# Reordering the opening of a cross-attention kernel: the first block's norm in two halves, mask rows on another queue, values in three row pairs

## The chip, the cores and the metric

The kernel runs on one core of a Trainium2 chip, as one program with one launch. The metric is the device time in microseconds (us), the median of several runs. The engines are TensorE (PE), VectorE (DVE), ScalarE (ACT), GpSimd (POOL) and SyncE (SP, which here only issues DMAs). Each works through its own list of instructions in order and waits on semaphores for the others.

## The reference

For x of 2048 tokens by 256 features and a context of 1601 rows by 192 features with a mask (float32 throughout):

```
xn  = layer_norm(x, g_norm)
q   = xn @ Wq                       # 16 heads of 64
k,v = split(context @ Wkv)          # 16 heads of 64
k,v = null key and value in front   # 1602 keys
s   = (q * scale) @ k^T, masked     # softmax over the keys
x   = x + layer_norm(softmax(s) @ v @ Wout, g_out)
h   = layer_norm(x), then three layers with weights of +1 or -1 (256 -> 1024 -> 1024 -> 256)
out = x + scaled h
```

## The kernel before

The sixteen heads are eight pairs (`NP`), the tokens four blocks of 512 (`NB`). The 32 units of the main loop (L681) are all pairs by all blocks, the block running fastest. A unit has 13 steps, one for each tile of 128 keys. A step makes scores for two heads on TensorE (L442), takes their exponential on ScalarE (`exps`, L468) and forms one chunk of the row maxima of the *next* unit (`max_chunk`, L376: two TensorE matmuls, L400, and one VectorE reduction, L403). GpSimd sums the exponentials into `acc` (L720, L722, L728). After the steps come the weighted values (L475), the output projection of the unit before, the query projection of the unit after next, and a part of the next pair's keys or values (L796): in blocks 0 and 1 the keys, in block 2 the first eight value tiles, in block 3 the last five. The feed-forward layers follow the last unit.

All this is under an order written out by hand. Each engine executes its instructions in the order in which the program text issues them. Two pools of PSUM buffers, `flex` and `spare`, have two buffers each of two banks; a new tile waits until the readers of the tile two back in its pool are done. `slot` alternates between the two pools by a counter, `n_slots`.

The opening (L566 to L678) has no unit before it to hide behind. It issues the loads, waits for the first block of x, norms it (`input_root` L538, `input_normed` L542, which centres four token tiles on VectorE at L91), turns it with eight transposes on TensorE (`input_turned`, L550) into `xnT`, and makes the first pair's keys (`first_keys`, L234, in four chunks), its queries (`first_queries`, L216, in two halves of 256 tokens) and its values (`values_begun` L300, `values_ended` L314). It then makes all 13 chunks of unit 0's maxima, combines them (`max_combined`, into `mcol`), turns them (`max_turned`, the matmul `mt` at L413), and starts the first exponential. `second_summed` and `second_normed` norm the second block of x on ScalarE and GpSimd. `keys_stepped` (L291) and `values_masked` (L360) work on the first pair's keys and values on GpSimd. `REST` is the last chunk of the maxima, of 66 keys for all four token tiles.

Before any data have landed, TensorE does 11 matmuls on the identity into a tile that nobody reads (`idle`, L633 to L635; 22 passes in the profile, since a float32 matmul shows as two). They wait for the identity, which GpSimd makes (`make_identity`, L580).

The context has 192 features: 128 in `ctx_a`, and the other 64 in `ctx_b`, held twice, in the lower and the upper 64 partitions. A matmul over 64 rows uses half of TensorE's rows, so two that use different halves (rows 0 to 63 and 64 to 127) and different banks run side by side: a row pair. (In the opening's timeline the 16 passes of eight value tiles over 128 rows, at 18.20, take 2.05 us, and the 16 passes over 64 rows as four such pairs, at 20.75, 1.05 us.) Value tile t takes its half by its bank, `(t - 8 * m) // 4`. The last five value tiles (8 to 12) lie with four in the first bank and one in the second, so one row pair and three single matmuls.

`keep` is the mask as one row on each partition, loaded with a broadcast; `kept` holds it by key tile; `masked_counted` (L425) sums it on TensorE into `spent`. `seen` (L708, L711) is a copy on ScalarE of one element of the last accumulator: after it, the exponentials of this unit need no wait of their own on GpSimd. It is made at step 2 in most units and at step 8 in the others:

```
if k == (2 if 2 < u < len(units) - 4 else 8) and last is not None:
    nc.scalar.copy(seen[:, 1:2], last[3][:1, 0, 0:1])
```

Of the kernel before, what the change touches and what calls it, by code (L numbers as in the profile page):

```python
# [21 lines left out]
CD = 192  # L22
# [16 lines left out]
def xattn_ffn(ctx, tc, x, ctxT, mask, g_norm, null_kv, wq, wkv, wout, g_out, k0, k1, k2, s0, s1, s2, out):  # L39
# [52 lines left out]


    norms = {}
    n_slots = 0

    def slot(name):
        nonlocal n_slots
# [49 lines left out]
    with ExitStack() as att:  # L148
# [19 lines left out]

        weights = {}

        def load_pair(p):
            wq_t = pp.tile([128, 2, 128], F32, tag="wq", name=f"wq_{p}")
            wa_t = pp.tile([128, 2, 128], F32, tag="wa", name=f"wa_{p}")
            wb_t = pp.tile([128, 2, 128], F32, tag="wb", name=f"wb_{p}")
            wo_t = lp.tile([128, D], F32, tag="wo", name=f"wo_{p}")
            both = wkv.rearrange("r (k w) -> r k w", k=2)[:, :, ts(p, 128)]
            nc.sync.dma_start(out=wa_t, in_=both[0:128])
            nc.sync.dma_start(out=wb_t[:64], in_=both[128:CD])
            nc.sync.dma_start(out=wb_t[64:], in_=both[128:CD])
            nc.sync.dma_start(out=wq_t, in_=wq[:, ts(p, 128)].rearrange("(c r) w -> r c w", c=2))  # L180
            if p > 0:
                nc.sync.dma_start(out=wo_t, in_=wout[ts(p, 128), :])
            weights[p] = (wq_t, wa_t, wb_t, wo_t)
# [50 lines left out]
        def first_keys(n, get, part=None):  # L234

            kT, _, kr = pairs[0]
            chunks = (CHUNKS[1], CHUNKS[2]) if n == 1 else (CHUNKS[n],)
            if part != 1:
                halves["k"] = get(f"psk_0_{n}")
            ps = halves["k"]  # L240
            for i, (start, w) in enumerate(chunks):
                if part is None or part == i:
                    nc.tensor.matmul(
                        ps[:, i, :w], weights[0][1][:, 0, :], ctx_a[:, ds(start, w)], start=True, stop=False
                    )
            if part == 0:
                return
            for i, (start, w) in enumerate(chunks):
                rows = ts(i, 64)
                nc.tensor.matmul(  # L250
                    ps[:, i, :w], weights[0][2][rows, 0, :], ctx_b[rows, ds(start, w)], start=False, stop=True
                )
            for i, (start, w) in enumerate(chunks):
                for part in range(2 if n == 0 else 1):
                    keys = ds(256 * part, 256) if n == 0 else ds(start, w)
                    relative(kT, ps[:, i, ts(part, 256)] if n == 0 else ps[:, i, :w], keys)
                    if n == 0 and part == 0:
                        nc.scalar.copy(kr[:, keys], kT[:, keys])
                    else:
                        nc.gpsimd.tensor_copy(kr[:, keys], kT[:, keys])  # L260
            if n == 3:
                nc.vector.memset(kT[:, KEYS:], 0.0)
# [34 lines left out]

        halves = {}

        def values_begun(p, m, tiles, get=flex):  # L300

            if (p, m) not in halves:
                halves[p, m] = get(f"psv_{p}_{m}").rearrange("p i (t d) -> p (i t) d", d=128)
            for t in tiles:
                nc.tensor.matmul(  # L305
                    halves[p, m][:, t - 8 * m, :],
                    ctx_a[:, ts(t, 128)],
                    weights[p][1][:, 1, :],
                    start=t % 4 == 0,
                    stop=False,  # L310
                    skip_group_check=True,
                )

        def values_ended(p, m):  # L314

            v, pv = pairs[p][1], halves[p, m]
            tiles = range(8 * m, min(8 * m + 8, KC))
            for t in sorted(tiles, key=lambda t: (t % 4, t)):
                rows = ts((t - 8 * m) // 4, 64)
                nc.tensor.matmul(  # L320
                    pv[:, t - 8 * m, :],
                    ctx_b[rows, ts(t, 128)],
                    weights[p][2][rows, 1, :],
                    start=False,
                    stop=True,
                    skip_group_check=True,
                )
            w = len(tiles)
            nc.scalar.copy(v[:, ds(8 * m, w), :], pv[:, :w, :])
            if p > 0 and m == 0:  # L330
                nc.gpsimd.tensor_copy(v[0:1, 0, :], nullv)

        def project_v(p, m):

            values_begun(p, m, range(8 * m, min(8 * m + 8, KC)))
            values_ended(p, m)

        def second_summed():

# [82 lines left out]
        def rows_of(k):  # L422
            return 128

        def masked_counted(get):  # L425

            ps = get("count")
            nc.tensor.matmul(ps[:, 0, :KC], ones_r.bitcast(F32), kept, start=True, stop=True)
            nc.vector.tensor_reduce(spent, ps[:, 0, :KC], AX.X, ALU.add)
            nc.gpsimd.tensor_scalar(spent, spent, float(KEYS), ident[:, KLAST : KLAST + 1], ALU.subtract, ALU.mult)  # L430
            for row in range(64, KLAST):
                nc.gpsimd.tensor_tensor(spent, spent, ident[:, row : row + 1], ALU.add)
# [105 lines left out]
        def input_root(b):  # L538
            mv = stats(x_sb[:, ts(b, 4), :], 4, f"x{b}")
            return mv, input_scale(b, mv)  # L540
# [35 lines left out]
            engine.dma_start(out=ctx_b[:64, ds(at + skip, w - skip)], in_=ctxT[128:CD, ds(at + skip - 1, w - skip)])  # L576


        nc.gpsimd.memset(keep[:, 0:1], 0)
        make_identity(nc, ident)  # L580
        nc.gpsimd.dma_start(out=gn_sb, in_=g_norm.rearrange("(c p) -> p c", p=128))
        for j in range(2):
            nc.gpsimd.dma_start(out=nullk[ts(j, DH), :], in_=null_kv[0].rearrange("(p o) -> p o", o=1))
        nc.gpsimd.dma_start(out=keep[:, 1:], in_=mask.partition_broadcast(128))
        for t in range(4):
            (nc.sync, nc.scalar)[t % 2].dma_start(out=x_sb[:, t, :], in_=x[ts(t, 128), :])
        load_context(nc.scalar, 0)
        load_pair(0)
        load_context(nc.sync, 1)
        at, w = CHUNKS[2]  # L590
        nc.sync.dma_start(out=ctx_a[:, ds(at, w)], in_=ctxT[0:128, ds(at - 1, w)])
# [34 lines left out]
        nc.scalar.activation(warm, eps_sb, AF.Sqrt)  # L626

        open_pair(0)
        xn = input_root(0)

        input_normed(0, *xn)

        idle = slot("idle")  # L633
        for _ in range(11):
            nc.tensor.matmul(idle[:, 0, :128], ident, ident, start=True, stop=True)  # L635
        input_turned(0, spare)
        first_keys(0, flex)
        first_queries(0)
        max_chunk(0, 0, 0)
        max_chunk(0, 0, 3)  # L640
        first_queries(1)
        nc.gpsimd.tensor_copy(kept[:, : KC - 1], mcol_u8[:, : KC - 1])
        nc.gpsimd.tensor_copy(kept[:KLAST, KC - 1 : KC], mcol_u8[:KLAST, KC - 1 : KC])
        mv, r = second_summed()
        max_chunk(0, 0, 6)
        first_keys(1, spare, 0)
        max_chunk(0, 0, 9)
        first_keys(1, spare, 1)
        values_begun(0, 0, range(0, 8), spare)
        max_chunk(0, 0, 1)  # L650
        nc.vector.reciprocal(r, r)
        second_normed(mv, r)
        nc.scalar.activation(warm, eps_sb, AF.Exp)
        max_chunk(0, 0, 4)
        values_ended(0, 0)
        max_chunk(0, 0, 7)
        first_keys(3, spare)
        max_chunk(0, 0, 10)
        values_begun(0, 1, range(8, KC), spare)
        max_chunk(0, 0, 2)  # L660
        values_ended(0, 1)
        max_chunk(0, 0, 5)
        keys_stepped(0)
        values_masked(0, 0)
        values_masked(0, 1)
        input_turned(1, spare)
        max_chunk(0, 0, 8)
        max_chunk(0, 0, 11)
        project_q(0, 1, spare)
        max_chunk(0, 0, REST)  # L670
        odd = spare("sT_0_0_1")
        sT = [spare("sT_0_0_0"), odd]
        scores(0, 0, 1, sT[1])
        max_combined(0, 0)
        max_turned(0, 0)
        scores(0, 0, 0, sT[0])
        masked_counted(flex)
        begin.__exit__(None, None, None)  # L678
        last = None
        with tc.manual_schedule():  # L680
            for u, (p, b) in enumerate(units):  # L681
# [25 lines left out]

                    nc.scalar.copy(seen[:, 0:1], before[:1, 0, 0:1])  # L708
                for k in range(KC):
                    if k == (2 if 2 < u < len(units) - 4 else 8) and last is not None:  # L710
                        nc.scalar.copy(seen[:, 1:2], last[3][:1, 0, 0:1])  # L711
                    if k == 0 and u > 0:

                        odd = spare(f"sT_{p}_{b}_1")
                        sT = [spare(f"sT_{p}_{b}_0"), odd]
                    es.append(exps(p, b, k, sT))
                    if nxt is not None:
                        max_chunk(*nxt, order[k])
                    if k == 2:
                        nc.gpsimd.tensor_tensor(acc, es[1], es[2], ALU.add)  # L720
                    elif 2 < k < 8:
                        nc.gpsimd.tensor_tensor(acc, acc, es[k], ALU.add)  # L722
# [231 lines left out]
```

## Time and profile before

| | |
|---|---|
| Runs | 1269.85, 1270.46, 1270.71 us |
| Median | 1270.46 us |
| Profiled execution | 1270.18 us, with a span of 1268.4 us |
| TensorE, GpSimd, VectorE, ScalarE busy | 99%, 80%, 60%, 57% of the span |
| First exponential of unit 0 | 34.65 us after the span's start |
| First exponential of unit 4, of unit 8 | 168.13, 300.19 us |

Times in the profile are counted from the start of the span. An engine's busy share is an average over the opening, the units and the feed-forward layers. In the timeline, a row's length runs from the start of the first of its instructions to the end of the last, and the number behind x counts them. Matmuls overlap, since one is issued before the one ahead of it has ended, so what an instruction costs TensorE is the distance between starts.

### The profile page before, as it was taken

How to read it: one execution, taken by the hardware profiler on the slowest of the kernel's cores; microseconds unless marked ns; L12 is line 12 of the kernel's file. 1: busy time of each engine (PE TensorE's matmuls, PEld its weight loads, DVE VectorE, ACT ScalarE, POOL GpSimd, SP SyncE). 2: the span in 40 equal slices, each digit the busy share in tenths (PEclk: the TensorE clock that was granted, in tenths of full speed). 3: DMA queues.
4: the chain of work that ended last, by engine and by line, in shares of the span. 5: the costliest groups of instructions: out<-in, count | busy, mean ns of one | idle time of the engine just before them, and what ended most of it. 6: DMA issues, size and time to landing. Idle time of an engine off the chain costs nothing.

```text
span 1268.4 us, 19642 instructions
## 1 busy us (share of the span) xinstructions
PE 1257.9 (99%) x8332; PEld 644.0 (51%) x8332; DVE 761.7 (60%) x812; ACT 717.9 (57%) x982; POOL 1008.5 (80%) x515
## 2 busy tenths in 40 slices
PE   8999999999999999999999999999999999999998
PEld 5344444444444444444444444444444443788887
DVE  6687766656665566556655666656666793635431
ACT  4776666666666656665666566666666676322120
POOL 5898999899889988998899988998898999701100
PEclk9999999999999999999999999999999999999999
DMA  6000000000000000000000000000000010000000
GB/s 171 1 1 5 1 1 13 5 1 1 13 5 1 1 14 5 1 1 13 5 1 2 13 5 1 1 1 6 1 17 1 1 42 1 1 17 1 17 17 17
DMA packets 16984, 13.46 MB, mean 11 GB/s; under 512 B 3152, under 2 KB 16336, under 8 KB 16896
## 3 DMA queue, kind: packets, MB, share of 16 engines
q1 hardware_dynamic: 15904, 11.21, 3.2%
q8 instruction: 65, 1.06, 0.4%
q10 hardware_dynamic: 656, 0.79, 0.2%
q0 software_dynamic: 336, 0.21, 0.1%
q14 instruction: 23, 0.19, 0.0%
HBM read 10.11 MB, written 2.10 MB: 10 GB/s over the span
## 4 chain that ended last, share of the span: by engine, by line
PE 95%; POOL 2%; ACT 1%; DMA 1%; issue 0%; DVE 0%; SPq 0%; DVEq 0%; POOLq 0%; ACTq 0%
PE sT L442 28%; PE av L475 27%; PE ps L836 12%; PE max L400 7%; PE psq L211 4%; PE po L488 4%; PE ps L867 2%; PE psv L305 2%; PE psk L270 1%; PE den L499 1%; PE sT L466 1%; PE psv L320 1%; POOL acc L728 1%; PE psk L275 1%; PE max L384 1%; PE mt L413 1%
## 5 line engine op out<-in xcount | busy, mean ns | idle before, releaser
L403 DVE TENSOR_REDUCE mx<-max 128x2 f32<-128x1024 f32 x384 | 444.4, 1218 | 86.0 <-PE max L400 82.3
L728 POOL TENSOR_TENSOR acc<-acc,e 128x1024 f32<-128x1024 f32 x192 | 473.1, 2464 | 15.1
L468 ACT ACTIVATE e<-sT 128x1024 f32<-128x1024 f32 x416 | 425.8, 1024 | 87.7 <-PE sT L466 44.3
L442 PE MATMUL sT<-qT,kT 64*128 64x512 f32 x1664 | 444.8, 608 | 1.6 <-ACT e L468 1.3
L722 POOL TENSOR_TENSOR acc<-acc,e 128x1024 f32<-128x1024 f32 x160 | 379.3, 2371 | 12.6
L475 PE MATMUL av<-e,v 128*32 128x512 f32 x3328 | 363.6, 592 | 0.1
L400 PE MATMUL max<-kr,qr 64*128 64x512 f32 x768 | 280.6, 718 | 1.2 <-ACT qr L227 1.0
L475 PEld LDWEIGHTS av<-e,v 128*32 128x32 f32 x3328 | 107.4, 110 | 237.9 <-issue 230.1
L442 PEld LDWEIGHTS sT<-qT,kT 64*128 64x128 f32 x1664 | 134.0, 185 | 132.6 <-ACT e L468 121.0
L720 POOL TENSOR_TENSOR acc<-e,e 128x1024 f32<-128x1024 f32 x32 | 75.6, 2363 | 59.6 <-ACT e L468 59.6
L400 PEld LDWEIGHTS max<-kr,qr 64*128 64x128 f32 x768 | 76.7, 187 | 88.6 <-DVE mx L403 65.2
L517 ACT COPY aoT<-r 32x256 f32<-32x256 f32 x224 | 90.2, 403 | 33.4 <-DVE r L511 31.1
L782 ACT COPY avs<-av 128x512 f32<-128x512 f32 x32 | 18.8, 587 | 145.8 <-PE av L475 145.8
L415 DVE TENSOR_TENSOR mT<-mt,pick 128x512 fp32r<-128x512 f32 x32 | 22.1, 690 | 113.4 <-PE mt L413 112.9
L518 DVE TENSOR_TENSOR aoT<-avs,aoT 128x512 f32<-128x512 f32 x28 | 33.3, 1189 | 94.4 <-ACT aoT L517 94.4
L836 PE MATMUL ps<-h0hi,w 128*128 128x512 f32 x256 | 79.6, 392 | 0.0
L836 PE MATMUL ps<-h0lo,w 128*128 128x512 f32 x256 | 78.9, 389 | 0.0
L124 POOL TENSOR_TENSOR y_sb<-y_sb,gout_sb 128x256 f32<-128x256 f32 x12 | 9.3, 777 | 85.6 <-DVE y_sb L91 85.6
L824 ACT ACTIVATE h1hi<-ps 128x1024 fp32r<-128x1024 f32 x16 | 16.4, 1027 | 99.2 <-PE ps L836 99.2
L212 ACT ACTIVATE qr<-psq 128x512 fp32r<-128x512 f32 x31 | 18.5, 598 | 93.5 <-PE psq L211 91.4
L488 PE MATMUL po<-wo,aoT 128*128 128x256 f32 x256 | 60.5, 379 | 0.0
L825 DVE SCALAR_TENSOR_TENSOR h1lo<-ps,h1hi 128x1024 fp32r<-128x1024 f32 x16 | 19.6, 1224 | 67.0 <-ACT h1hi L824 67.0
(171 smaller groups left out, 1207.8 us busy)
## 6 DMA issues: line engine op xcount, KB each, us to landing
out_x<-o SPq DMA_DIRECT2D x7, 256.0 KB, 2.1
x_sb<-in_x SPq DMA_DIRECT2D x3, 512.0 KB, 5.2
wa<-in_wkv SPq DMA_DIRECT2D x8, 128.0 KB, 2.9
wb<-in_wkv SPq DMA_DIRECT2D x16, 64.0 KB, 2.5
wq<-in_wq SPq DMA_DIRECT2D x8, 128.0 KB, 2.2
wo<-in_wout SPq DMA_DIRECT2D x8, 128.0 KB, 2.1
xnT<-in_k SPq DMA_DIRECT2D x1, 1024.0 KB, 5.7
ctx_a<-in_ctxT SPq DMA_DIRECT2D x2, 256.0 KB, 6.2
```

The lines of the kernel that those rows point to most:

```text
L211: nc.tensor.matmul(ps[:, 0, :], weights[p][0][:, c, :], xnT[:, b, c, :], start=c == 0, stop=c == 1)
L400: nc.tensor.matmul(ps[:, j, :w], qr[rows, ts(t, 128)], kr[rows, ds(start, w)], start=True, stop=True)
L403: nc.vector.tensor_reduce(maxima[p, b][:, t, :, c], ps[:, :, :w], AX.X, ALU.max)
L442: nc.tensor.matmul(ps[:n, j, :], kT[rows, ds(128 * KEY_TILES[k], n)], qT[rows, :], start=k < 2, stop=k >= 2, skip_group_check=k >= 2,)
L468: nc.scalar.activation(e, ps, AF.Exp)
L475: nc.tensor.matmul(av[ts(i, 32), 0, :], v[:n, KEY_TILES[k], ts(i, 32)], e[:n, i // 2, :], start=k == 1, stop=k == 0, tile_position=(0, 32 ...
L488: nc.tensor.matmul(pv[:, t, :], aoT[:, ts(t, 128)], weights[p][3], start=True, stop=True)
L517: nc.scalar.copy(aoT[ds(64 * j + 32 * rows, 32), ts(h, 256)], r[ds(64 * j + 32 * h, 32), :])
L720: nc.gpsimd.tensor_tensor(acc, es[1], es[2], ALU.add)
L722: nc.gpsimd.tensor_tensor(acc, acc, es[k], ALU.add)
L728: nc.gpsimd.tensor_tensor(acc, acc, es[k], ALU.add)
L836: nc.tensor.matmul(ps[:, f, :], w(c)[:, ts(2 * g + f, 128)], parts[part][:, c, :], start=i == 0, stop=i == len(steps) - 1,)
```

## The change

Six things are done, nearly all in the opening.

- GpSimd issues the loads of `gn_sb` and `nullk` ahead of the identity. The mask rows `keep` go from GpSimd's queue to SP's, behind the first half of the weights. Token tiles 2 and 3 of x are loaded after the first chunk of the context and most of pair 0's weights.
- The first block is normed and turned in two halves of two token tiles (`first_stats`, `first_centred`, `first_turned`). The first keys' first part stands ahead of the transposes in TensorE's list. The second half's reciprocal and centred tiles stand behind `max_chunk(0, 0, 0)` on VectorE; ScalarE does both scalings of its transposes.
- In the opening's second part, the chunks of keys, values and maxima are interleaved in another way; the Exp table is loaded after the first copy of values; REST comes before the second block's query projection.
- The last five value tiles lie as three and two in the two banks (`places`), for every pair: two row pairs and a single matmul. (In the opening too; the edit's name for it is three row pairs.) Their copy on ScalarE becomes two, of three tiles and of two.
- The count of the mask goes into the second bank of the last keys' tile, right behind them, rather than into a `flex` tile at the end.
- The `seen` copy of unit 28 is made at step 2 rather than 8. `n_slots` starts at 1 and `idle` is a `flex` tile, so `slot` alternates as it did.

The diff, with the definitions of two loads cut:

```
-    n_slots = 0
+    n_slots = 1
...
-            if part != 1:
+            if not part:
                 halves["k"] = get(f"psk_0_{n}")
...
-            if part == 0:
+            if part in (0, 1):
                 return
...
+        places = {t: t if t < 8 else t - 8 if t < 11 else t - 7 for t in range(KC)}
...
-            for t in sorted(tiles, key=lambda t: (t % 4, t)):
-                rows = ts((t - 8 * m) // 4, 64)
+            for t in sorted(tiles, key=lambda t: (places[t] % 4, t)):
+                rows = ts(places[t] // 4, 64)
...
-            w = len(tiles)
-            nc.scalar.copy(v[:, ds(8 * m, w), :], pv[:, :w, :])
+            for at, w in ((0, 8),) if m == 0 else ((8, 3), (11, 2)):
+                nc.scalar.copy(v[:, ds(at, w), :], pv[:, ds(places[at], w), :])
...
+        def first_stats(h):
+            mv = stats(x_sb[:, ts(h, 2), :], 2, f"x0{h}")
+            r = sp.tile([128, 4], F32, tag="rstd", name=f"rstd_x0{h}")
+            nc.scalar.activation(r[:, :2], mv[:, :2, 1], AF.Sqrt, bias=eps2_sb, scale=1.0 + EPS)
+            return h, mv, r
+        def first_centred(h, mv, r):
+            nc.vector.reciprocal(r[:, :2], r[:, :2])
+            for j in range(2):
+                centred(y_sb[:, 2 * h + j, :], x_sb[:, 2 * h + j, :], mv, r, j)
+        def first_turned(h):
+            pt = spare(f"xT_0_{h}")
+            cols = ts(h, 256)
+            for j in range(2):
+                for c in range(2):
+                    nc.tensor.transpose(pt[:, c, ts(j, 128)], y_sb[:, 2 * h + j, ts(c, 128)], ident)
+            nc.scalar.mul(xnT[:, 0, 0, cols], pt[:, 0, :256], gn_sb[:, 0:1])
+            if h == 0:
+                nc.vector.tensor_scalar_mul(xnT[:, 0, 1, cols], pt[:, 1, :256], gn_sb[:, 1:2])
+            else:
+                nc.scalar.mul(xnT[:, 0, 1, cols], pt[:, 1, :256], gn_sb[:, 1:2])
...
-        def masked_counted(get):
-            ps = get("count")
-            nc.tensor.matmul(ps[:, 0, :KC], ones_r.bitcast(F32), kept, start=True, stop=True)
-            nc.vector.tensor_reduce(spent, ps[:, 0, :KC], AX.X, ALU.add)
+        def masked_counted(ps):
+            nc.tensor.matmul(ps[:, 1, :KC], ones_r.bitcast(F32), kept, start=True, stop=True)
+            nc.vector.tensor_reduce(spent, ps[:, 1, :KC], AX.X, ALU.add)
...
-        nc.gpsimd.memset(keep[:, 0:1], 0)
-        make_identity(nc, ident)
         nc.gpsimd.dma_start(out=gn_sb, in_=g_norm.rearrange("(c p) -> p c", p=128))
         for j in range(2):
             nc.gpsimd.dma_start(out=nullk[ts(j, DH), :], in_=null_kv[0].rearrange("(p o) -> p o", o=1))
-        nc.gpsimd.dma_start(out=keep[:, 1:], in_=mask.partition_broadcast(128))
-        for t in range(4):
-            (nc.sync, nc.scalar)[t % 2].dma_start(out=x_sb[:, t, :], in_=x[ts(t, 128), :])
+        nc.gpsimd.memset(keep[:, 0:1], 0)
+        make_identity(nc, ident)
+        for t, engine in enumerate((nc.sync, nc.scalar)):
+            engine.dma_start(out=x_sb[:, t, :], in_=x[ts(t, 128), :])
+        load_pair(0, 0)
         load_context(nc.scalar, 0)
-        load_pair(0)
+        nc.sync.dma_start(out=keep[:, 1:], in_=mask.partition_broadcast(128))
+        load_pair(0, 1)
+        for t, engine in ((2, nc.sync), (3, nc.scalar)):
+            engine.dma_start(out=x_sb[:, t, :], in_=x[ts(t, 128), :])
+        load_pair(0, 2)
...
-        xn = input_root(0)
-        input_normed(0, *xn)
-        idle = slot("idle")
+        idle = flex("idle")
         for _ in range(11):
             nc.tensor.matmul(idle[:, 0, :128], ident, ident, start=True, stop=True)
-        input_turned(0, spare)
-        first_keys(0, flex)
+        first_centred(*first_stats(0))
+        first_keys(0, flex, 0)
+        first_turned(0)
+        first_keys(0, flex, 2)
         first_queries(0)
+        later = first_stats(1)
         max_chunk(0, 0, 0)
+        first_centred(*later)
         max_chunk(0, 0, 3)
+        first_turned(1)
         first_queries(1)
...
+        first_keys(1, spare, 0)
         mv, r = second_summed()
         max_chunk(0, 0, 6)
-        first_keys(1, spare, 0)
+        first_keys(1, spare, 1)
         max_chunk(0, 0, 9)
-        first_keys(1, spare, 1)
-        values_begun(0, 0, range(0, 8), spare)
+        first_keys(1, spare, 2)
+        values_begun(0, 0, range(0, 6), spare)
         max_chunk(0, 0, 1)
-        nc.vector.reciprocal(r, r)
-        second_normed(mv, r)
-        nc.scalar.activation(warm, eps_sb, AF.Exp)
+        values_begun(0, 0, range(6, 8), spare)
         max_chunk(0, 0, 4)
         values_ended(0, 0)
+        nc.scalar.activation(warm, eps_sb, AF.Exp)
         max_chunk(0, 0, 7)
         first_keys(3, spare)
+        masked_counted(halves["k"])
         max_chunk(0, 0, 10)
-        values_begun(0, 1, range(8, KC), spare)
+        nc.vector.reciprocal(r, r)
+        second_normed(mv, r)
         max_chunk(0, 0, 2)
-        values_ended(0, 1)
+        values_begun(0, 1, range(8, KC), spare)
         max_chunk(0, 0, 5)
+        values_ended(0, 1)
         keys_stepped(0)
         values_masked(0, 0)
         values_masked(0, 1)
-        input_turned(1, spare)
         max_chunk(0, 0, 8)
+        input_turned(1, spare)
         max_chunk(0, 0, 11)
-        project_q(0, 1, spare)
         max_chunk(0, 0, REST)
+        project_q(0, 1, spare)
...
-        masked_counted(flex)
...
-                    if k == (2 if 2 < u < len(units) - 4 else 8) and last is not None:
+                    if k == (2 if 2 < u < len(units) - 3 else 8) and last is not None:
```

In the built program, the loads of pair 1's first weights (`wa`) come third on SP's list, ahead of the mask rows.

## The prediction

> **What bounds the kernel now.** I read the page's busy shares first, then the chain that ended last, then the waits of TensorE in the opening, the timeline of the opening, and last the stretches of ScalarE where a new pair of heads begins. One part of the page's first section and its chain:
>
> ```profile
> PE 1257.9 (99%) x8332; PEld 644.0 (51%) x8332; DVE 761.7 (60%) x812; ACT 717.9 (57%) x982; POOL 1008.5 (80%) x515
> PE 95%; POOL 2%; ACT 1%; DMA 1%; issue 0%; DVE 0%; SPq 0%; DVEq 0%; POOLq 0%; ACTq 0%
> ```
>
> TensorE is busy 99% of the span, and the chain runs over it for 95%. So an edit counts if it takes passes off TensorE or closes one of its few gaps, and it costs if it opens one. The granted clock is 1.00 all along. The waits of TensorE between 6 and 35 us (columns: total, times, longest):
>
> ```profile
> PE xT L556 <- DVE y_sb L91: 1.1, 1, 1.1
> PE max L400 <- ACT qr L227: 1.0, 2, 0.6
> PE psv L305 <- ACT v L329: 0.3, 1, 0.3
> PE mt L413 <- DVE mcol L408: 0.3, 1, 0.3
> PE max L400 <- DVE mx L403: 0.2, 1, 0.2
> ```
>
> These 2.97 us are all that a better order could close there: 1.14 at the first transposes, 0.57 before the first maxima (11.33 to 11.89), 0.47 at 14.16, 0.20 at 22.00, 0.33 at 24.03, 0.26 at 32.50. The rest of the opening is passes. Its timeline (start, length, engine, line, instruction, and in brackets the idle time before and its releaser):
>
> ```profile
> 1.03 0.29 POOL masks.py:199 TENSOR_SCALAR_AFFINE_SELECT ident<-ident 128x128 f32<-128x128 f32 x1
> 1.38 4.20 PE L635 MATMUL idle<-ident 128*128 128x128 f32 x22 [1.38 <-POOL ident masks.py:199]
> 1.50 0.98 POOL L581 DMA_DIRECT2D gn_sb<-in_g_norm  x1 [0.18 <-issue]
> 2.49 1.08 POOL L583 DMA_DIRECT2D nullk<-in_null_kv  x2
> 6.71 1.43 PE L556 MATMUL xT<-ident,y_sb 128*128 128x128 f32 x8 [1.14 <-DVE y_sb L91]
> 8.12 1.10 PE L243 MATMUL psk<-ctx_a,wa 128*128 128x512 f32 x2
> 9.14 1.12 PE L250 MATMUL psk<-ctx_b,wb 64*128 64x512 f32 x2
> 12.43 3.50 DVE L403 TENSOR_REDUCE mx<-max 128x2 f32<-128x1024 f32 x3 [1.19 <-PE max L400]
> 12.56 1.13 PE L226 MATMUL psq<-xnT,wq 128*128 128x256 f32 x4
> 28.76 1.98 PE L211 MATMUL psq<-xnT,wq 128*128 128x512 f32 x4
> 32.50 0.30 PE L413 MATMUL mt<-ident,mcol 128*128 128x128 f32 x1 [0.26 <-DVE mcol L408]
> ```
>
> The identity is ready at 1.3 because GpSimd makes it before its DMAs; the idle passes that wait for it end at 5.58, over a microsecond before anyone needs TensorE. From 8.12 on TensorE is nearly unbroken until mt at 32.50 and the first exponential at 34.65.
>
> **The opening's front.** After the change GpSimd issues gn (0.98) and the two nullk loads (1.08) before the identity: +2.06. The 22 idle passes start at 1.38 + 2.06 = 3.44 and, at their 4.20, end at 7.64. They stand first in TensorE's queue, so what the two halves free before 8.1 is mostly spent on them. Behind them stand psk_0's first part (1.03 from its start to the next matmul), four of the eight transposes, and psk_0's second part. The eight transposes took 1.43, paced by the four centred tiles (1.41); four ready ones I take at 0.5. So psk_0's second part starts at 7.64 + 1.03 + 0.5 = 9.17, against 9.14: the early half of the norm gains about nothing. I take -0.1, since it now follows ready data. Bounds: -0.8, if psk_0 could start where the first context chunk lands (7.27 in the trace), to +1.6: TensorE's clock. Listed one by one, the idle passes are 0.213 apart until 4.31, 2.93 after the first, and 0.112 after; if the slow pace held to the end, 22 x 0.213 = 4.69 put it 0.5 later, and psk_0's first part would double (+1.03).
>
> The Trainium skill ("TensorE: Matmul & The Clock Gate", Part 1: The HAM clock gate) says that TensorE runs at half rate until some 3.4 us of activity, in a window that runs freely. That speaks against a late identity: by the page the fast pace would come up to 0.48 later than this trace's 2.93, which makes the idle passes end about 0.2 later. With it the opening's sum would be 0.2 longer.
>
> **The second half's norm.** Its two statistics fit VectorE's 1.19 of idle before the first reduction (two took 1.1). But its reciprocal and two centred tiles stand behind the first reduction: 12.43 + 1.14 (spacing of the three in 3.50) = 13.57, reciprocal 0.2, two tiles at 0.35: ready at 14.5. TensorE, done with max_3 at about 12.5, waits for them, then does the transposes (end 14.8), and the second query projection waits for ScalarE's copy (0.45, between the 256-wide copy's 0.38 and 0.7 for two). It starts at 15.2 in place of 12.56: +2.65. Queued behind it are psk_1's first part and max_6, and so VectorE's reduction of max_6, with 2 us of idle. Both sides: +1.5, if the tiles were ahead of the reduction; +3.2, if both copies count.
>
> **The second part.** (a) TensorE's later waits, 0.47 + 0.20 + 0.33 + 0.26 = 1.26, go, since data then are ready before it; the value copy no longer stands behind the Exp table load (1.28 at 21.58). What is late next is TensorE's own queue. Bounds: -1.26 to 0. (b) The count, one matmul of 0.32, leaves the end (33.79) and stands behind psk_3, in its second bank. It waits for VectorE's step on psk_3, which comes behind two reductions; before, that step began 1.0 after psk_3 ended (23.22 to 24.19), and max_10 now stands behind the wait: I take +0.8 (0 to 1.3), the pass itself moving at no cost. (c) The projection of the next block (1.98) moves behind REST: mt now waits in TensorE's queue for it, but those passes were ahead of REST before, so only the order changes: 0, covered by VectorE's last reductions; without that cover, +1.2 to +1.8 (REST's end to mt is 1.2 now, then 3.0). (d) Five values' tiles in 6 passes, not 8: -0.22. (e) The mask rows on SP's queue wait there for a GpSimd memset (about 2.9 us, behind its DMAs), with half of wb, wq, x2 and the later chunks behind them; pair 1's first weights (128 KB) also come up to third place. Later landings slip some 0.5; ctx_b's chunks were needed at 17.14, with landings up to 13.7, and x block 1 (16.20) feeds only ScalarE's sums. 0; 0.5 if that cover goes.
>
> Opening: -0.1 + 2.65 - 1.26 + 0.8 - 0.22 = **+1.9**.
>
> The Trainium skill ("DMA: Bandwidth & Descriptors", Issuing engines are not separate DMA queues) gives no gain to a transfer for being moved to another issuer. The trace has the mask rows landing at 8.79, before their first reader at 10.36, so the sum has no gain for it either.
>
> **The 32 units.** The diff reaches them in two places. *Three row pairs*: each of the seven later pairs ends its values with these ctx_b passes, and TensorE goes from them straight to the scores. ScalarE there, and in unit 28:
>
> ```profile
> 827.33 0.69 ACT L329 COPY v<-psv 128x640 f32<-128x640 f32 x1 [1.11 <-PE psv L320]
> 828.05 0.19 ACT L708 COPY seen<-e 1x1 f32<-1x1 f32 x1
> 828.49 1.02 ACT L468 ACTIVATE e<-sT 128x1024 f32<-128x1024 f32 x1 [0.25 <-PE sT L466]
> ```
> ```profile
> 960.55 1.02 ACT L468 ACTIVATE e<-sT 128x1024 f32<-128x1024 f32 x1 [0.25 <-PE sT L466]
> 963.24 1.94 ACT L468 ACTIVATE e<-sT 128x1024 f32<-128x1024 f32 x2 [0.41 <-PE max L400]
> 969.89 0.17 ACT L711 COPY seen<-acc 1x1 f32<-1x1 f32 x1
> ```
>
> The eight passes take 0.99 there (826.14 to 827.13), so two fewer at 0.11 to 0.12 are 0.22 a pair: 7 x 0.22 = -1.54. The cover: the first exponential waits 0.25 for TensorE. The one copy of 640 (0.69) becomes 384 and 256, some 0.49 + 0.38 by the 256- and 512-wide copies (0.38, 0.60), so ScalarE is done 0.18 later after its matmuls, less than the 0.25. If that cover failed: 0. *Unit 28* takes its `seen` copy at step 2, not 8. Its first to last exponentials start 14.29 apart (960.55 to 974.84), those of unit 24 13.88 (828.49 to 842.37): -0.4, between 0 and -0.41; the accumulator that it reads was done at 961.95, before that step.
>
> Sum against the profiled execution's 1270.18 (span 1268.4 and 1.8 around it): 1270.18 + 1.9 - 1.54 - 0.4 = 1270.1. The median, 1270.46, lies 0.28 above that execution, so 1270.4.
>
> **Rivals.** *One, faster: the opening gets no longer but shorter.* TensorE's five waits from 11.33 on (1.83) go and none comes; transposes of the second half cost their 0.5; the values give 0.22: -1.5, and 1270.46 - 1.5 - 1.94 = 1267.0. For it: less data ahead of the first keys, the value copy before the table load, and 1.2 to 2 us of VectorE idle to use. Against: the second half's centred tiles stand behind a reduction by program order. It decides where psq's second half starts by 12.6 + 0.4. 0.27. *Two, slower: the reductions take the lead.* max_6's reduction starts at about 17.9, not 14.70 (+3.2), the count adds 0.8, and if VectorE recovers none of it REST is that late too, with psq_1 behind it (+1.8 by (c)): +5.8 - 0.2, so 1270.46 + 5.6 - 1.94 = 1274.1. For it: thirteen reductions of 1.22 are a chain of their own. Against: they show 3.17 of idle after the first (0.27, 0.92, 0.97, 0.26, 0.21, 0.54), to be used up. It decides from 4.5 us lost in the opening. 0.16. *Three, the units do not change*: ScalarE's second copy takes the 0.22 back seven times: 1270.4 + 1.54 = 1271.9. For it: 0.07 of cover is thin. 0.12. The forecast has the other 0.45.
>
> **The numbers.** 0.2%, 2.5 us, is about what a measurement of this kernel can tell from no change. Forecast and rival three lie within it: 0.57; faster 0.27, slower 0.16. The range, 1266.9 to 1273.0, takes in rival one's price and, above rival three, the front's upper bound, and leaves out rival two. The likeliest case's own range is 1268.6 to 1272.0.
>
> **What would show it.** Right: identity near 3.4, idle passes ending at 7.5 to 7.9, a TensorE wait of over a microsecond for y_sb at about 13, another at the count, first exponential at 36.0 to 37.0; units 3, 7, ... 27 shorter by 0.2, unit 28 by 0.4. Wrong: a first exponential before 35 or after 38, or unit lengths as they were.

## The result and the profile after

The changed kernel takes 1274.19 us (median of 13 runs, 1271.15 to 1275.24) against 1270.24 for the kernel before, run beside it. The ratio is 1.0026, with a 95% interval of 1.0018 to 1.0035: slower by a quarter of a percent, where 1270.4 was forecast and 1273.0 was the end of the range. The profiled execution took 1274.18, with a span of 1272.4. The 13 runs fall into two groups, and each run's granted TensorE clock tells them apart: three at 1271.15 to 1271.27 with a mean clock of 1.00, ten at 1273.8 to 1275.2, nine of them with 0.997 and one (1273.83) with 0.999. The profile is of the second kind.

The page, in the lines shown of before, and the row of the granted clock (each digit a fortieth of the span, in tenths, 9 being full):

```profile
PE 1258.0 (99%) x8332; PEld 643.9 (51%) x8332; DVE 758.8 (60%) x813; ACT 719.5 (57%) x993; POOL 1007.5 (79%) x514
PEclk8999999999999999999999999999999999999999
PE 92%; POOL 5%; issue 1%; DVE 1%; ACT 0%; DVEq 0%; POOLq 0%; ACTq 0%
```

TensorE's busy time and its number of passes are as they were, and the other engines' busy times differ by at most 2.9 us. The one new digit in the clock's row is the 8 at the left. The waits of TensorE between 6 and 41 us:

```profile
PE xT L372 <- DVE y_sb L91: 1.6, 1, 1.6
PE psk L468 <- DVE kT L245: 0.9, 1, 0.9
PE max L441 <- POOL kept L687: 0.6, 1, 0.6
PE psq L239 <- ACT xnT L373: 0.6, 1, 0.6
PE max L441 <- POOL kr L273: 0.3, 1, 0.3
PE max L425 <- DVE mx L444: 0.2, 1, 0.2
```

They sum to 4.1, where before there were 1.83 after the first transposes. The largest is the one that the prediction named, the second half's tiles behind the first reduction. The opening's timeline:

```profile
1.27 0.99 POOL L619 DMA_DIRECT2D gn_sb<-in_g_norm  x1 [0.84 <-POOLq L990]
3.68 0.29 POOL masks.py:199 TENSOR_SCALAR_AFFINE_SELECT ident<-ident 128x128 f32<-128x128 f32 x1
4.03 4.47 PE L675 MATMUL idle<-ident 128*128 128x128 f32 x22 [4.03 <-POOL mcol_u L655]
9.73 1.12 PE L263 MATMUL psk<-ctx_b,wb 64*128 64x512 f32 x2
14.81 1.11 PE L372 MATMUL xT<-ident,y_sb 128*128 128x128 f32 x4 [1.60 <-DVE y_sb L91]
16.49 2.07 PE L239 MATMUL psq<-xnT,wq 128*128 128x256 f32 x4 [0.56 <-ACT xnT L373]
```

The first row shows GpSimd's first load starting at 1.27, not at 0.72 where its first instruction was before: the idle passes start 0.6 later than worked out. The last row is the surprise: the same four passes that took 1.13 before take 2.07. A table by stretches of 3.4 us (length, busy time of TensorE, its weight loads, VectorE, ScalarE, GpSimd, then the granted clock, the DMA engines' share and their GB/s) shows why:

```profile
11.10:14.50 3.40, 1.55 (x8) 0.72 (x6) 3.18 (x9) 1.36 (x4) 0.67 (x3) 1.00 1.08 245
14.50:17.90 3.40, 2.52 (x7) 1.85 (x8) 1.72 (x3) 0.84 (x2) 0.00 (x0) 0.51 1.13 266
17.90:21.30 3.40, 3.40 (x7) 1.33 (x6) 0.26 (x1) 2.58 (x10) 0.00 (x0) 0.50 0.83 247
21.30:24.70 3.40, 3.40 (x18) 1.83 (x18) 2.93 (x4) 2.70 (x9) 0.26 (x2) 0.99 0.65 154
```

TensorE works 1.55 of the 3.40 us around the new wait, and at 14.56 its clock is halved. It stays so until 21.38, though from 16.49 on TensorE has no gap. The first exponential comes at 40.50, 5.85 later than before, in place of the 1.9 forecast:

```profile
40.50 1.94 ACT L508 ACTIVATE e<-sT 128x1024 f32<-128x1024 f32 x2 [1.60 <-PE sT L506]
```

The units did as forecast. ScalarE at the first exponential of a new pair, and in unit 28:

```profile
831.86 0.76 ACT L344 COPY v<-psv 128x384 f32<-128x384 f32 x2 [0.89 <-PE psv L335]
833.02 1.02 ACT L508 ACTIVATE e<-sT 128x1024 f32<-128x1024 f32 x1 [0.19 <-PE sT L506]
```
```profile
967.05 0.17 ACT L758 COPY seen<-acc 1x1 f32<-1x1 f32 x1
967.23 10.04 ACT L508 ACTIVATE e<-sT 128x1024 f32<-128x1024 f32 x9
```

The two copies take 0.76 in a row, not 0.87, and the exponential still waits for TensorE (0.19). From first exponential to first exponential, each of the seven units before a new pair is 0.21 to 0.23 shorter (32.84 to 32.62 for unit 3), and unit 28 by 0.40 (31.23 to 30.83): 1.53 and 0.40, together 1.93, so that 5.85 shrinks to 3.92 by the last unit. In unit 28 the gap of 0.41 before the third exponential is gone.

### The profile page after: what moved, and what is told of

It is laid out like the page before. It is cut to its first block, busy times and chain, and to the rows that moved or that the text cites. A ratio compares the mean times of both kernels' runs of the same rounds, so it can differ in the third digit from the quotient of the medians.

```text
span 1272.4 us, 19653 instructions
## 1 busy us (share of the span) xinstructions
PE 1258.0 (99%) x8332; PEld 643.9 (51%) x8332; DVE 758.8 (60%) x813; ACT 719.5 (57%) x993; POOL 1007.5 (79%) x514
## 4 chain that ended last, share of the span: by engine, by line
PE 92%; POOL 5%; issue 1%; DVE 1%; ACT 0%; DVEq 0%; POOLq 0%; ACTq 0%
PE sT L482 27%; PE av L515 26%; PE ps L883 12%; PE max L441 7%; PE psq L224 4%; PE po L528 4%; PE ps L914 2%; POOL acc L775 2%; POOL acc L769 2%; PE psv L320 2%; PE psk L283 1%; PE den L539 1%; PE sT L506 1%; PE psv L335 1%; PE psk L288 1%
```

## The experiments

Each was timed beside the kernel before, whose medians were between 1270.5 and 1270.6. Since a run with a halved clock costs whole microseconds and only some runs have one, the times are given as a median and as the time of the runs at full clock (1.00 as recorded), which is nearest to what the order of the work alone costs.

**The units alone** (`units_only`). The kernel before, with the changed `places`, `values_begun` and `values_ended`, and:

```
-                    if k == (2 if 2 < u < len(units) - 4 else 8) and last is not None:
+                    if k == (2 if 2 < u < len(units) - 3 else 8) and last is not None:
```

> The kernel before with its own opening, and only what the diff does to the values' last tiles (two row pairs, copy in two) and to unit 28. Theory 1 (the units give 7 x 0.22 + 0.40 = 1.94 us and the whole loss lies in the opening): 1268.2 to 1268.4 us against 1270.2, each unit before a new pair 0.22 shorter, the granted clock 1.00. Rival (the units gain only because the opening left the engines shifted): 1270 us.

Measured: 1268.43 (ratio 0.9983, 0.9974 to 0.9991), clock 1.00 in nine of eleven runs. In its profile the way from the first exponential of unit 0 to that of unit 31 is 1.76 shorter than before (1.93 in the changed kernel), so the two edits gain with the old opening as well.

**The front or the second part.** `second_part` is the changed kernel with the first loads in the order of before, one norm over four tiles (`input_root`, `input_normed`) and these lines of before:

```
-        first_centred(*first_stats(0))
-        first_keys(0, flex, 0)
-        first_turned(0)
-        first_keys(0, flex, 2)
+        input_turned(0, spare)
+        first_keys(0, flex)
         first_queries(0)
-        later = first_stats(1)
         max_chunk(0, 0, 0)
-        first_centred(*later)
         max_chunk(0, 0, 3)
-        first_turned(1)
         first_queries(1)
```

> The loads and the front of the kernel before (one norm, eight transposes, keys, queries), and from there on the changed kernel: its order of the second part, the count in the spare bank, the values and unit 28. Theory 1 (the loss is the front's): the first exponential within 0.5 of 34.65, 1268.4 us (1268.0 to 1269.0), the clock as steady as in the kernel before. Rival (the second part's order loses too: the count's wait of 0.85 and the query projection behind the last maxima): first exponential 1 to 2 us later, 1269.5 to 1270.3 us.

Measured: 1268.31 (0.9984, 0.9975 to 0.9992); the first exponential at 34.62. `front_only` is the other half: the changed loads and front, and from there on the order of before, with the count at the end:

```
-        first_keys(1, spare, 0)
         mv, r = second_summed()
         max_chunk(0, 0, 6)
+        first_keys(1, spare, 0)
...
         scores(0, 0, 0, sT[0])
+        masked_counted(flex)
```

> The changed kernel's loads and front, then the second part of the kernel before (old order, count at the end), and the units as changed. Theory 1: the loss of the changed kernel stays, 1271 us where the clock is full and 1274 where it is halved for 6.8 us, and most runs are of the second kind, since the wait of 1.6 us for the second half is in it. Rival: close to the 1268.4 us of the kernel before with the changed units.

Measured: 1276.71, worse than the changed kernel; one of six runs at full clock, 1271.08, the others at 0.994 to 0.996. In its profile the clock is halved from 14.71 to 28.36, twice as long as in the changed kernel's; why so long was not found. So the whole loss is the front's. The second part is worth nothing either way (1268.31 with it, 1268.43 without it in `units_only`). The waits of TensorE in `second_part` (window 5 to 41, leaving out the first transposes and the first unit's own) say why:

```profile
PE psk L468 <- DVE kT L245: 0.9, 1, 0.9
PE max L441 <- ACT qr L240: 0.6, 1, 0.6
PE max L441 <- POOL kr L273: 0.4, 1, 0.4
PE max L425 <- DVE mx L444: 0.2, 1, 0.2
```

They sum to 2.1, against 1.83 of before: three of the old waits go (0.47, 0.33 and 0.26), and the count and the keys' rounding on GpSimd take their place.

**The wait filled** (`filler`).

```
             pt = spare(f"xT_0_{h}")
+            if h == 1:
+                for _ in range(6):
+                    nc.tensor.matmul(pt[:, 0, :128], ident, ident, start=True, stop=True)
```

> The changed kernel with 6 more matmuls on the identity (12 passes, about 1.3 us at the fast pace) in the second half's tile, ahead of its transposes, where TensorE waits 1.60 us for y_sb. Nothing else moves. Theory 1 (TensorE's idle time of 0.56 and 1.60 us around 12 to 14.8 us is what halves its clock from 14.6 to 21.4): the clock stays at 1.00 in all runs and every run takes 1271.2 us, as the three undisturbed runs of the changed kernel did. Rival (the clock falls for a reason of its own, such as the chip or the load of the DMAs): still 0.997 in most runs, 1274.2 us.

Measured: the fall of 6.8 us is gone. Three runs take 1271.24 to 1271.27 at full clock, the other eight 1272.3 to 1272.9 at 0.999; none is at 0.997, while `ident_first` below, which keeps the wait (and opens one more), has 0.997 in eight of twelve. In its profile, which is of one of the three, the same two stretches:

```profile
11.10:14.50 3.40, 2.80 (x19) 1.89 (x17) 3.18 (x10) 1.36 (x4) 0.67 (x3) 1.00 1.08 251
14.50:17.90 3.40, 2.80 (x12) 1.56 (x12) 1.44 (x2) 1.70 (x6) 0.00 (x0) 1.00 1.13 244
```

Twelve passes of no use, which delay nothing, take 1.7 us off the median (1274.19 to 1272.52). They also show the price of the order by itself: this profile, at full clock until its last matmul, has its first exponential at 37.56, 2.91 after the kernel before:

```profile
37.56 1.94 ACT L511 ACTIVATE e<-sT 128x1024 f32<-128x1024 f32 x2 [1.59 <-PE sT L509]
```

**The rest of the falls** (`filler_count_end`). The same with the count in the old place and the old tile:

```
-        masked_counted(halves["k"])
...
         scores(0, 0, 0, sT[0])
+        masked_counted(flex)
```

> The changed kernel with the 6 filler matmuls, and the count as in the kernel before: a matmul in a tile of flex at the end, with no wait in the middle. With the fillers 8 of 11 runs still had a clock of 0.999 and took 1272.6, the others 1271.24. Theory 1 (the rest is the count's wait of 0.85, which with the idle time around it sits in one window of the clock's): clock 1.00 in nearly all runs, and 0.3 to 0.8 us less than 1271.24 for the wait itself. Rival (the short fall of the clock comes from elsewhere, the waits near 12 us or the late idle passes): still 0.999 in most runs.

Measured: 1271.36, from 1270.64 to 1272.11, with no second group; the clock is 0.999 or 1.00, and in the profile (0.999) the part that is missing lies at the end, from 1267.97 on, behind the last matmul (1265.76), not in the opening. So without the count's wait of 0.85 the second group is gone. That a shorter fall can follow this wait is seen in two other profiles: each has a fall of 3.41 right behind the 3.41 us that hold it (from 26.78 on in `halves_old_loads`, from 32.78 on in `ident_first`). The 0.3 to 0.8 us expected for the wait itself did not come; the fastest run is 0.6 below 1271.24, the median 0.1 above. The spread that is left was not looked into.

**The wait alone** (`gap_in_before`). The kernel before, with nothing of the change:

```
         max_chunk(0, 0, 3)
+        held = wp.tile([128, 256], F32, tag="held", name="held", bufs=1)
+        for _ in range(13):
+            nc.scalar.copy(held, x_sb[:, 0, :])
         first_queries(1)
```

> The kernel before with nothing of the change, but 13 copies of 128 x 256 more on ScalarE ahead of its work on the second half of the queries (into a tile nobody reads), so that TensorE waits some 2 us near 14 us rather than 0.47. Theory 1 (a window of 3.4 us in which TensorE works less than half of the time halves its clock for 3.4 or 6.8 us): 1271 to 1272 us where the clock stays, for the wait itself, and 1274 or more with a clock of 0.997 in most runs. Rival (the halved clock belongs to the changed loads or to the late start of the idle passes): the clock stays at 1.00, 1271 to 1272 us.

Measured: 1276.48 in the median of five runs; four at 0.996 or 0.997, one at 0.999 (1275.11). The wait became 4.2 us rather than the 2 that was meant, so its own price is larger, and it empties one stretch wholly. After it (same columns):

```profile
14.10:17.50 3.40, 0.00 (x0) 0.00 (x0) 0.80 (x1) 3.15 (x9) 0.00 (x0) 1.00 1.13 258
17.50:20.90 3.40, 2.90 (x6) 0.96 (x6) 1.23 (x1) 2.93 (x12) 0.25 (x1) 0.52 0.81 241
20.90:24.30 3.40, 3.40 (x6) 1.11 (x8) 1.23 (x1) 3.25 (x10) 0.00 (x0) 0.50 0.81 189
24.30:27.70 3.40, 3.40 (x28) 2.50 (x26) 1.60 (x3) 0.64 (x2) 1.22 (x2) 0.98 0.03 7
```

So a wait of TensorE is enough to halve the clock in a kernel whose loads and idle passes are the old ones, and the rival that the changed loads are needed for it falls. It is no test of a wait as short as the changed kernel's; that one is `filler`, which keeps the changed loads.

**The identity first** (`ident_first`). In the changed kernel:

```
+        nc.gpsimd.memset(keep[:, 0:1], 0)
+        make_identity(nc, ident)
         nc.gpsimd.dma_start(out=gn_sb, in_=g_norm.rearrange("(c p) -> p c", p=128))
...
-        nc.gpsimd.memset(keep[:, 0:1], 0)
-        make_identity(nc, ident)
```

In the built program pair 1's weights then go back to their old place on SP's list.

> The changed kernel with GpSimd's old order at the start: identity first, then the loads of gn and nullk. Theory 1: the idle passes start at 1.4 in place of 4.03 and end by 5.6, so psk_0 starts where its data land, about 7.2 in place of 8.34: the front is 1.1 us earlier, 1270.1 us where the clock stays; the wait of 1.6 us for y_sb remains, so the clock may still be halved (1273.1). Rival (the front is bound by the landings, not by the identity): psk_0 still near 8.3, and no change of time.

Measured: 1273.18; of three runs at full clock two take 1270.4 and one 1271.1, and eight of twelve are at 0.997. So the front is at best 0.8 cheaper, and psk_0 starts at 8.11, only 0.2 earlier than in the changed kernel: it waits for wa, which lands at 7.97 rather than 6.26. The mask rows no longer wait for GpSimd and are issued at 1.91, not 3.50; that they hold up wa is likely but not shown.

```profile
PE psk L256 <- DMA wa<-in_wkv: 2.1, 1, 2.1
```

The front is held from two sides, by the idle passes in the one order and by the landings in the other. In this profile, a run of 1277.23, the early end of the idle passes opened a wait of its own and the clock was halved from 8.89 to 22.55.

**The second half normed early.** `normed_early`, in the changed kernel:

```
         first_centred(*first_stats(0))
+        first_centred(*first_stats(1))
...
-        later = first_stats(1)
         max_chunk(0, 0, 0)
-        first_centred(*later)
```

> The changed kernel with the second half's statistics, reciprocal and centred tiles right behind the first half's on VectorE (in its idle time of 4.25 us before 10.34), not behind the first reduction. Theory 1: the wait of 1.60 us for y_sb goes, and with it the halved clock: the clock 1.00, max_6 about 2 us earlier than with the full clock, 1269.5 us (1269.0 to 1270.2). Rival (the reductions, not this wait, set the end of the opening): about 1271 us at a clock of 1.00. Second rival (the clock falls for its own reason): 0.997 still.

Measured: 1271.97; six of twelve runs at full clock, 1270.85 to 1271.7, and five still at 0.996 or 0.997 (1273.9 to 1275.7). So the second rival came in part: the wait for y_sb is not the only thing that brings the long fall, and what brought it in these five was not seen, since the profile is of a run at full clock. In it the wait for y_sb is gone from TensorE, but the gain is 0.4 at best, not the 1.7 expected: tile 2 of x lands at 9.35 in this order, so its statistics run at 9.4 and push the first half's own scaling on VectorE to 11.76 and its keys to 12.16. `halves_old_loads` is the same kernel with the loads and GpSimd's start of before:

```
-        for t, engine in enumerate((nc.sync, nc.scalar)):
-            engine.dma_start(out=x_sb[:, t, :], in_=x[ts(t, 128), :])
-        load_pair(0, 0)
+        for t in range(4):
+            (nc.sync, nc.scalar)[t % 2].dma_start(out=x_sb[:, t, :], in_=x[ts(t, 128), :])
...
```

> The changed kernel with the loads and GpSimd's start of the kernel before (identity first, four tiles of x first, mask rows on GpSimd's queue), and the second half's statistics, reciprocal and centred tiles right behind the first half's on VectorE: x tiles 2 and 3 land near 4.2 there, not 9.3. The halves, the reordered second part, the count, the values and unit 28 stay. Theory 1 (the loss is the late load of half the tokens and the late identity): no wait of 1.6 us; but psk_0 waits for its weights (about 8.0), and all eight transposes (1.0) and ScalarE's scalings (0.5) come after it, where the kernel before had them ahead of it for nothing: 1269.5 us (1269.2 to 1270.2) at a clock of 1.00. Rival (the halves gain, as the change has it, once the loads are right): 1268.3 or less. Second rival (order of the loads is worth nothing): 1271.

Measured: 1272.03 in the median; the three fastest take 1269.1 to 1269.7 (at 0.999), as expected, and five of twelve are at 0.993 or 0.994 (1275.3 to 1276.6). So with the old loads the halves still cost about 1 us against `second_part`, and the falls stay: TensorE, by its profile, now waits 1.7 us for wa between the idle passes and psk_0. Which wait brought the long falls of the five runs was not seen, since the profile is of another run.

**The loads alone** (`new_loads`). `second_part`, with the changed loads and GpSimd's changed start:

```
-        for t in range(4):
-            (nc.sync, nc.scalar)[t % 2].dma_start(out=x_sb[:, t, :], in_=x[ts(t, 128), :])
+        for t, engine in enumerate((nc.sync, nc.scalar)):
+            engine.dma_start(out=x_sb[:, t, :], in_=x[ts(t, 128), :])
+        load_pair(0, 0)
...
```

> The changed kernel's loads and GpSimd's start, with the front of the kernel before: one norm over four tiles, eight transposes, then keys and queries. Second part, values and unit 28 as changed. Theory 1: tiles 2 and 3 of x land at 9.3, so the eight transposes end near 12 and psk_0 with them, 4 us later than in the kernel before: 1272 us at a full clock, and with TensorE idle from 8.5 to 11 the clock is halved in most runs (1275 and more). Rival (the loads' order does not matter): 1268.4 to 1269.

Measured: 1273.66 in the median of five runs, the fastest 1272.19; two at 0.996, the other three at 0.998 or 0.999. The first transposes wait until 11.07, and the clock is halved from 12.40 to 22.64.

**Two versions that keep what works.** `units_table` is `units_only` with two lines changed.

```
-        for _ in range(11):
+        for _ in range(15):
             nc.tensor.matmul(idle[:, 0, :128], ident, ident, start=True, stop=True)
...
-        nc.scalar.activation(warm, eps_sb, AF.Exp)
         max_chunk(0, 0, 4)
         values_ended(0, 0)
+        nc.scalar.activation(warm, eps_sb, AF.Exp)
```

> The kernel before with its own loads and front, the changed values and unit 28, and two small things: 15 idle matmuls in place of 11, to fill the 1.14 us that TensorE waits at 5.58, and the Exp table load behind the first copy of values (from the change). Theory 1: the values' copy no longer holds TensorE (0.33 at 24.03), 1268.1 us, and the falls of the clock are rarer than the 2 in 11 of the kernel with the changed units alone. Rival: neither wait is worth anything since the reductions follow, 1268.4.

Measured: 1268.12 (0.9981, 0.9972 to 0.9989), the best of all, with the narrowest spread, 1267.80 to 1268.65, against 1268.0 to 1270.5 for `units_only`; its first exponential is at 34.27. Against `units_only` its median is 0.3 less, within that kernel's spread. `second_part_idle` is `second_part` with the same first edit:

```
-        for _ in range(11):
+        for _ in range(15):
             nc.tensor.matmul(idle[:, 0, :128], ident, ident, start=True, stop=True)
```

> The loads and the front of the kernel before with 15 idle matmuls in place of 11, and everything from the second part on as in the changed kernel. Theory 1: as the better of its two parents, 1268.1 us, the clock at 1.00 or 0.999 in all runs. Rival (the second part and the longer idle stretch each save on their own): 1267.7.

Measured: 1268.55 (0.9984, 0.9975 to 0.9992). No gain over `second_part`.

## Why the prediction was wrong

Right, by its steps: the values' passes (-1.53 for -1.54), unit 28 (-0.40 for -0.4), no collision in ScalarE's copies, so rival three did not come; the wait for y_sb (1.60 at 14.81), the wait of the count (0.85 for 0.8), the loads of SP that nothing waits for in the second part. Rival two, the reductions in the lead, did not come either: at full clock the opening loses 2.9, not 5.6. That the median, 1274.19, meets this rival's 1274.1, and that the profiled opening's 5.85 is past its mark of 4.5, is chance: in that profile VectorE stands idle for 4.82 us before the reduction of max_6 at 21.04, waiting for TensorE at half pace.

Two things failed.

*The step that took the clock for settled.* The prediction wrote "The granted clock is 1.00 all along" and weighed the clock only in the opening's front, as a late start of the fast pace, for at most 1.6 us. It did not ask what a wait of its own making does to the clock. The changed kernel's wait, with those beside it, halves the clock for 6.8 us in the profile, and nine of thirteen runs have that profile's mean clock of 0.997. `filler` takes that fall away by giving TensorE work without use, and `gap_in_before` brings such a fall about with nothing but a (longer) wait. Its price is the distance between the two groups, 1274.2 - 1271.2 = 3.0 us: passes that took 1.13 took 2.07. The upper end of the range would have had to be about 1275.

The Trainium skill ("TensorE: Matmul & The Clock Gate", Part 1: The HAM clock gate) has the mechanism: a free-running window of 3413 ns after which the clock is set by how busy TensorE was. The runs agree with the window: 14.56 to 21.38 is 6.82, twice 3.41; 8.89 to 22.55 in `ident_first` is four times 3.41. They disagree with the condition that this part of the page gives for falling back, an idle window: here TensorE was busy for 44% of the 3.41 us up to 14.56 (1.50 us), and what was measured decides. A window that runs freely may also split the same wait over two, which would give the two groups; that is not shown, since no run of the changed kernel at full clock was profiled.

*The size of the front's term at full clock*: -0.1 + 2.65 in the prediction. By the profile of `filler`, the second half's projection starts at 15.87, 3.31 after the 12.56 of before, where the two terms give 2.55. Of the 0.76 between them 0.4 is the front: the idle passes start at 4.03, not 3.44, because GpSimd's first load starts at 1.27, and psk_0's second part at 9.45 in that profile, 0.3 later than before where -0.1 was taken. The rest, 0.35, is the second half itself: its four transposes (0.76 for 0.5) and ScalarE's scalings (0.56 for 0.45). The second term, -1.26 for waits that go and +0.8 for the count, -0.22 for the passes, was to give back 0.7; it gave 0.4, from 3.31 to 2.91, and in `second_part` 0.03 (34.62 for 34.65). With 2.91 the sum is 1270.24 + 2.91 - 1.93 = 1271.2, which is what the three runs at full clock show; the point forecast missed those by 0.8.

What of the front is whose, at full clock: the halves with the old loads 1269.1 to 1269.7 (at 0.999), about 1 above `second_part` (transposes and scalings that cost nothing in the kernel before, where wa lands at 7.9 and the transposes end at 8.1, now come after psk_0's first part); the late loads and identity another 1.1 to 1.8 (1270.85, the fastest of `normed_early`); the tiles behind the reduction 0.4 at most, since 1271.2 lies within the 1270.85 to 1271.7 of `normed_early`.

Still open: which measure of activity the clock goes by. In the first 45 us, counted in stretches of 3.41 us from the recorded changes of the clock, the five stretches at full clock in which TensorE was busy for at most 44% were each followed by a fall (0% in `gap_in_before`, 39% in `ident_first`, 41% in `front_only` and in `new_loads`, 44% in the changed kernel), and the seven with 51 to 71% were not, two of them in the kernel before. But of the seven at 75%, each with the count's wait in it, two were (at 32.8 in `ident_first`, at 26.8 in `halves_old_loads`) and five were not (in the changed kernel, `filler`, `new_loads`, `second_part` and `second_part_idle`), so the busy share alone does not decide. And after 8.89 in `ident_first`, and after 12.40 in `new_loads`, TensorE was busy throughout the next 3.4 us without getting its clock back.

## What to carry to other kernels

A wait of TensorE can cost more than its length: where waits left it busy for 44% or less of one of the clock's stretches of 3.41 us, the next two to four stretches ran at half pace here. Price a wait with the passes behind it at half pace, and look at the granted clock of single runs, not only of the profile at hand. Before moving work ahead of a landing, see what the engine already does for free during it; here eight transposes were hidden behind the weights' landing, and splitting them brought them out. Small edits in a loop that is bound all along, such as two passes fewer in each pair, are the ones whose sum held: to a hundredth in the changed kernel (1.93 for 1.94), to 0.2 in `units_only` (1.76).

## What the runs showed of the hardware

- The recorded granted clock does not show the slow start. In the changed kernel the idle passes are 0.213 us apart until 7.6, under a clock recorded as 1.00, and 0.112 after; in the later fall, recorded as 0.50, the transposes are again 0.213 apart.
- The fast pace came 3.1 us after the first idle pass in the kernel before (the prediction's 2.93 leaves out one more slow pass), between 2.9 and 4.4 us after it in eight other profiles, and in the remaining five not before the idle passes had ended, some 5 us after the first. So it can come later by much more than the 0.48 that the prediction allowed, and a front that depends on it varies by itself.
- The clock came back after multiples of 3.41 us only: 3.41, 6.82, 10.24 and 13.66 us.
- GpSimd's load of gn as its first instruction began at 1.27; a memset in the same place began at 0.72.
